# Inner weight sums split between GpSimd and VectorE, wide sums in other slots, and layer 1 mixed by ScalarE and GpSimd, in a two-level Strassen-Winograd kernel

## The chip, the cores and the metric

The kernel runs on one core of a Trainium2 chip. The metric is the time of one execution on the device in microseconds, lower is better; a kernel's time is the median of its runs. The profile is one more execution of the same program.

## The reference

The input x is 2 x 2048 x 512 in float32. Two layers are added to it, one after the other:

```python
def _L0_cond_ref(x, type_label, wi, wo, swi, swo, g1, g2):
    s0 = relu(x @ swi[0]) @ swo[0]
    s1 = relu(x @ swi[1]) @ swo[1]
    eo = relu(x @ wi[type_label]) @ wo[type_label]      # one of 3 experts per batch row
    gate_in = concat([eo[:, 0], s0[:, 0], s1[:, 0]], axis=-1)
    w = softmax(relu(gate_in @ g1) @ g2, axis=-1)       # 3 numbers per batch row
    return eo * w[0] + s0 * w[1] + s1 * w[2]

def _L1_cond_ref(x, cat_ids, W, b):
    return x @ W[cat_ids] + b[cat_ids]                  # one of 64 matrices per batch row

x = x + _L0_cond_ref(x, ...)
x = x + _L1_cond_ref(x, ...)
```

wi and swi are 512 x 2048, wo and swo 2048 x 512, g1 is 1536 x 512, g2 512 x 3, W 512 x 512. The gate reads the first row of a sequence alone.

## The kernel before

**Units.** The 4096 rows are cut into four blocks of 1024. A unit is one pair (weight set, block): units 0 to 3 are the first shared pair of matrices on blocks 0 to 3, units 4 to 7 the second, units 8 and 9 the expert of batch row 0 on blocks 0 and 1, units 10 and 11 the expert of row 1 on blocks 2 and 3. Every unit has an *up* half (x times wi, then relu, kept in SBUF as four quadrants H) and a *down* half (H times wo).

**Two levels of seven products.** Both halves use a Winograd variant of Strassen's method at two levels. At the outer level there are seven products i. Operand 1, 2 and 4 of a side are plain quadrants, 3, 5, 6 and 7 are sums of quadrants. Inside each product the same scheme is applied again with seven inner products k. In the up half an inner product is two slots (d = 0 and 1) of two matmuls each, in the order of `SEQ_UP`: x1 x1 y5 y5 x6 x6 z2 x7 x7 z2 x4 x4 y3 y3; the letter names the PSUM bank that it accumulates into. So an up half has 7 x 14 = 98 slots and a down half 7 x 7 = 49 slots of four matmuls each (`SLOTS_DN`). The outer order is 1, 6, 2, 5, 7, 4, 3 in an up half (1, 2, 6, 5, 7, 4, 3 in unit 0) and 1, 2, 3, 7, 6, 5, 4 in a down half. After a slot, VectorE or ScalarE takes what it needs out of the bank: a seed of z after x1 (`uz`, L614 and L616), a snapshot after x6 and x7 (`us`, L620 and L622; the bank goes on being accumulated, so x7 must wait for the snapshot of x6), results after the rest. Products 6, 2, 7, 4 and 3 add to a quadrant that is there already, on VectorE; 1 and 5 store, mostly on ScalarE.

**Sums beside the matmuls.** All of these are issued from one program in a fixed order (`tc.manual_schedule`), so each engine has a queue in program order:

- `x_sums` (L277 and L291, GpSimd): the sums of x of one product, made while the product before it runs.
- `wide` (L580 in product 7, L585 in product 4, VectorE): four sums of 128 x 1024 per product that add one quadrant of H to another; L585's results then get their relu on ScalarE.
- `make_tops` (L539 to L546) and `outer_sum` (L691), VectorE: sums of H for the down half.
- `prep_w` (L132, GpSimd): sums of weights of the next matrices. The seven matrices that follow the first one are prepared, one queued per unit in units 0 to 6. A matrix goes in four groups g: 1 MB is loaded into the one buffer `raw` (L165), four sums make `s` (outer sums, plain inner quadrants), four make `o` (plain outer, inner sums), four more make `t` from `s` (both), and each of the three is stored to DRAM (1 MB, tensors `ws`, L182), three steps later. `raw`, `s`, `o` and `t` have one buffer each.
- `fetch_w` (L374 to L393, SP): fetches weights of 256 KB, 12 ahead of their use, in order. Products of plain quadrants come from the inputs, others from `ws`. If the matrix is still being prepared, `ready` first issues all that is left of the preparation.

The background work is stepped from the slots: `paced(prep_bg, RATE_UP[n > 0][j])` and `paced(other_bg, 0.5)` after each up slot, 0.05 and 1 after each down slot.

**Layer 1 and the gate.** After unit 8 and after unit 10, `gate` computes the softmax weights (27 steps on `other_bg`). After units 8, 9 and 10, `layer1` is queued for the block just finished: it loads w1 (1 MB, L855) and the bias row (2 KB, `brow`, L857), multiplies the row by ones (`pb`, L865), and then handles eight tiles of 128 rows. Per tile it loads x and the three results (`mix`, four DMAs of 256 KB), adds the three with their gates on VectorE (L910), does four matmuls (`po`, L875) and adds the bias (L883). The `mix` tiles use the buffers raw, o and t in turn. The last block is done by `premix`, queued at the beginning of the last down half: it loads `acc` (2 MB) and four parts of 1 MB (`pm`, L939; the fourth when the first part's sums are issued), then weights and bias as above, then 16 sums (L947). At slot 47 of 49 what is left of it is issued at once; `last_mix` and `last_layer1` follow.

Of the kernel before, what the change touches and what calls it, by code (L numbers as in the profile page):

```python
# [32 lines left out]
def cond_resid_kernel(  # L33
# [101 lines left out]
    def prep_w(e, kind, eng):  # L135
# [3 lines left out]
        late = []  # L139

        def tick():
            for job in list(late):
                job[0] -= 1
                if job[0] <= 0:
                    job[1]()
                    late.remove(job)

        def load(g):
            t = bigp.tile([P, 2048], F32, tag="raw", bufs=1, name=f"pr_{e}_{kind}_{g}")
# [16 lines left out]
            return t  # L166

        raws = {0: load(0)}
        for _ in range(6):
            yield  # L170
        for g in range(NG):
            new = lambda part: bigp.tile(
                [P, 2048], F32, tag=part, bufs=1, name=f"p{part}_{e}_{kind}_{g}"
            )
            raw = raws[g].rearrange("p (a b c d f) -> p a b c d f", a=2, b=2, c=2, d=2)
            ts, to, tt = new("s"), new("o"), new("t")
            vs = ts.rearrange("p (s b d f) -> p s b d f", s=4, b=2, d=2)
            vo = to.rearrange("p (a c s f) -> p a c s f", a=2, c=2, s=4)
            vt = tt.rearrange("p (n s f) -> p n s f", n=4, s=4)

            def store(part, t, g=g):
                nc.sync.dma_start(  # L182
                    out=ws[e, kind, part][:, :, g * P : (g + 1) * P],
                    in_=t.rearrange("p (n f) -> p n f", n=16),
                )

            place = lambda n: SLOT_A[n] - 4
            for _ in sums_a(eng, lambda r, c: raw[:, r, :, c, :, :], lambda n: vs[:, place(n)]):
                tick()
                yield  # L190
            late.append([3, lambda t=ts, put=store: put("s", t)])
            for _ in sums_a(
                eng, lambda r, c: raw[:, :, r, :, c, :], lambda n: vo[:, :, :, place(n), :]
            ):
                tick()
                yield
            late.append([3, lambda t=to, put=store: put("o", t)])
            if g + 1 < NG:
                raws[g + 1] = load(g + 1)
# [6 lines left out]
        while late:  # L206
            tick()
            yield
# [874 lines left out]
```

## Time and profile before

| | |
|---|---|
| median of 3 runs | 2398.66 us (2397.9 to 2400.77) |
| the profiled execution | 2391.57 us |
| its span, first to last instruction | 2389.8 us |
| mean granted TensorE clock in it | 0.978 |
| DMA | 541.40 MB, mean 227 GB/s |

How to read it: PE is TensorE's matmuls, PEld its weight loads, DVE VectorE, ACT ScalarE, POOL GpSimd, SP the engine that issues nearly all DMAs (SPq is its queue). A line of the waits has the waiting engine and line, what it waited for, the sum in us, the number of times and the longest. A line of the windows has the stretch in us from the span's start, its length, the busy time and count of PE, PEld, DVE, ACT and POOL, the granted clock, the DMA engines' busy share and GB/s. A line of a timeline has the start, the duration, the engine, the line, the operation, output and inputs, shapes and count, and in brackets the idle time before it and what ended it. Each matmul of 32-bit floats has two records.

Unit n's halves in the span, read from the first and last matmul of each (us):

| unit | up from | down from | up | down |
|---|---|---|---|---|
| 0 | 15.5 | 147.5 | 131.5 | 93.0 |
| 1 | 240.4 | 335.2 | 95.0 | 88.7 |
| 2 | 423.7 | 516.5 | 92.9 | 89.6 |
| 3 | 605.9 | 697.1 | 91.4 | 85.3 |
| 4 | 782.3 | 877.5 | 95.3 | 85.3 |
| 5 | 962.6 | 1057.7 | 95.2 | 85.3 |
| 6 | 1142.8 | 1233.6 | 91.0 | 85.3 |
| 7 | 1318.7 | 1411.1 | 92.6 | 84.8 |
| 8 | 1495.7 | 1588.8 | 93.3 | 85.3 |
| 9 | 1674.0 | 1796.4 | 122.6 | 110.4 |
| 10 | 1906.7 | 2040.2 | 133.7 | 84.8 |
| 11 | 2124.8 | 2233.5 | 108.9 | 124.7 |

After unit 11 the last eight tiles of layer 1 take 31.6 us more. A half without any wait has 392 records of 0.216 us, 84.7 us; a tile of layer 1 adds 3.46 us. The up halves of units 9 and 11 hold three tiles of layer 1 and their down halves five, the up half of unit 10 holds eight.

### The profile page before, as it was taken

How to read it: one execution, taken by the hardware profiler on the slowest of the kernel's cores; microseconds unless marked ns; L12 is line 12 of the kernel's file. 1: busy time of each engine (PE TensorE's matmuls, PEld its weight loads, DVE VectorE, ACT ScalarE, POOL GpSimd, SP SyncE). 2: the span in 40 equal slices, each digit the busy share in tenths (PEclk: the TensorE clock that was granted, in tenths of full speed). 3: DMA queues.
4: the chain of work that ended last, by engine and by line, in shares of the span. 5: the costliest groups of instructions: out<-in, count | busy, mean ns of one | idle time of the engine just before them, and what ended most of it. 6: DMA issues, size and time to landing. Idle time of an engine off the chain costs nothing.

```text
span 2389.8 us, 28294 instructions
## 1 busy us (share of the span) xinstructions
PE 2232.5 (93%) x9808; PEld 1870.1 (78%) x9808; DVE 1725.6 (72%) x2082; ACT 500.4 (21%) x833; POOL 930.3 (39%) x774
## 2 busy tenths in 40 slices
PE   6879999989999999989999999999889989998979
PEld 5668888878878878878878878888666866886655
DVE  6857687587687687687687687687577557768755
ACT  3211221221221221221221321221221112112100
POOL 5932741741841861661841752752600320032000
PEclk9989999999999999999999999999999999999999
DMA  7775976976975985785975985785866565576662
GB/s 293 251 251 189 287 242 191 294 218 196 325 243 152 303 254 172 255 260 178 306 228 170 286 267 182 255 279 166 285 200 216 163 209 187 184 246 187 201 216 75
DMA packets 489784, 541.40 MB, mean 227 GB/s; under 512 B 25000, under 2 KB 326056, under 8 KB 486060
## 3 DMA queue, kind: packets, MB, share of 16 engines
q1 hardware_dynamic: 488588, 537.50, 70.4%
q10 hardware_dynamic: 1056, 2.10, 0.2%
q8 instruction: 80, 1.31, 0.2%
q14 instruction: 60, 0.49, 0.1%
HBM read 400.04 MB, written 139.46 MB: 226 GB/s over the span
## 4 chain that ended last, share of the span: by engine, by line
PE 66%; POOL 14%; DVE 9%; DMA 7%; issue 2%; SPq 2%; ACT 0%; POOLq 0%; ACTq 0%; DVEq 0%
PE dx L720 22%; PE ux L599 13%; PE dy L720 11%; PE uy L599 6%; PE dz L720 5%; PE po L875 5%; POOL ps L132 3%; POOL xi L291 3%; POOL po L132 3%; PE uz L599 3%; POOL pt L132 2%; DVE mix L910 1%; POOL x L277 1%; DMA xn<-in_x_dram 1%; DMA ws_t<-pt 1%
## 5 line engine op out<-in xcount | busy, mean ns | idle before, releaser
L599 PE MATMUL ux<-xi,w 128*128 128x256 f32 x1984 | 494.2, 391 | 72.7 <-issue 33.4
L599 PEld LDWEIGHTS ux<-xi,w 128*128 128x128 f32 x1984 | 382.9, 195 | 147.2 <-issue 53.0
L291 POOL TENSOR_TENSOR xi<-x 128x256 f32<-128x256 f32 x120 | 125.6, 1047 | 951.8 <-PE dx L720 928.2
L720 PE MATMUL dx<-t,w 128*128 128x256 f32 x1728 | 410.9, 381 | 1.7 <-DVE ds L742 1.5
L720 PEld LDWEIGHTS dx<-t,w 128*128 128x128 f32 x1728 | 328.0, 191 | 51.0 <-DVE ds L742 4.5
L622 DVE TENSOR_TENSOR us<-ux,h 128x512 f32<-128x512 f32 x240 | 162.4, 685 | 118.2 <-PE ux L599 118.1
L691 DVE TENSOR_TENSOR h<-h,h 128x1024 f32<-128x1024 f32 x192 | 229.1, 1217 | 0.0
L575 ACT ACTIVATE h<-h 128x1024 f32<-128x1024 f32 x156 | 164.7, 1056 | 294.5 <-DVE h L585 135.9
L633 ACT ACTIVATE h<-uz 128x512 f32<-128x512 f32 x168 | 99.5, 592 | 483.2 <-PE uz L599 458.2
L627 DVE TENSOR_TENSOR h<-uy,us 128x512 f32<-128x512 f32 x168 | 115.7, 691 | 89.9 <-ACT us L620 85.5
L599 PE MATMUL uy<-xi,w 128*128 128x256 f32 x672 | 162.3, 385 | 6.0 <-POOL xi L291 6.0
L720 PE MATMUL dx<-h,w 128*128 128x256 f32 x672 | 160.3, 382 | 0.5 <-DMA w<-in_L_cond_swo_dram 0.5
L720 PE MATMUL dy<-h,w 128*128 128x256 f32 x672 | 158.9, 379 | 0.5 <-DVE y L744 0.5
L720 PE MATMUL dz<-h,w 128*128 128x256 f32 x672 | 158.8, 379 | 0.0
L646 DVE TENSOR_TENSOR h<-uy,us 128x512 f32<-128x512 f32 x168 | 114.9, 690 | 56.9 <-PE uy L599 55.8
L599 PEld LDWEIGHTS uy<-xi,w 128*128 128x128 f32 x672 | 130.1, 194 | 26.1 <-POOL xi L291 6.4
L132 POOL TENSOR_TENSOR ps<-pr 128x512 f32<-128x512 f32 x56 | 81.8, 1471 | 168.7 <-DMA pr<-in_L_cond_wo_dram 49.0
L720 PEld LDWEIGHTS dx<-h,w 128*128 128x128 f32 x672 | 128.4, 192 | 19.3 <-issue 1.0
L720 PEld LDWEIGHTS dy<-h,w 128*128 128x128 f32 x672 | 127.4, 190 | 18.9 <-issue 1.0
L720 PEld LDWEIGHTS dz<-h,w 128*128 128x128 f32 x672 | 127.4, 190 | 17.2
L720 PE MATMUL dy<-t,w 128*128 128x256 f32 x576 | 136.1, 379 | 0.0
L599 PE MATMUL uz<-x,w 128*128 128x256 f32 x464 | 123.4, 390 | 0.0
(133 smaller groups left out, 3446.1 us busy)
## 6 DMA issues: line engine op xcount, KB each, us to landing
w<-ws_t SPq DMA_DIRECT2D x368, 256.0 KB, 3.4
w<-ws_s SPq DMA_DIRECT2D x282, 256.0 KB, 2.9
w<-ws_o SPq DMA_DIRECT2D x276, 256.0 KB, 3.7
ws_s<-ps SPq DMA_DIRECT2D x28, 1024.0 KB, 6.4
ws_o<-po SPq DMA_DIRECT2D x28, 1024.0 KB, 7.2
ws_t<-pt SPq DMA_DIRECT2D x28, 1024.0 KB, 7.1
ys<-y SPq DMA_DIRECT2D x11, 2048.0 KB, 7.9
w<-in_L_cond_swo_dram SPq DMA_DIRECT2D x72, 256.0 KB, 2.9
```

The source lines that it names most:

```text
L132: eng.tensor_tensor(o, i0, i1, op)
L277: eng.tensor_tensor(o[:, b], i0[:, b], i1[:, b], SUB)
L291: eng.tensor_tensor(s(k), i0, i1, SUB)
L575: nc.scalar.activation(v, v, AF.Relu)
L599: nc.tensor.matmul(p[:, g, :], lhsT=wt[:, 2 * d + g, :], rhs=x_ops[n, i, k], start=first and g == 0, stop=True, skip_group_check=True,)
L622: nc.vector.tensor_tensor(t, p, half(src, 12 if k == 6 else 22, d), ADD)
L627: nc.vector.tensor_tensor(half(dst, 22, d), bank["y", d], t, ADD)
L633: nc.scalar.activation(half(dst, 11, d), p, AF.Relu if i in final else AF.Copy)
L646: nc.vector.tensor_tensor(half(dst, 12, d), p, sn["b", d], ADD)
L691: nc.vector.tensor_tensor(bl(o), bl(i0), bl(i1), SUB)
L720: nc.tensor.matmul(p, lhsT=wt[:, g, :], rhs=op[g], start=first and g == 0, stop=True, skip_group_check=True,)
L875: nc.tensor.matmul(po[t], lhsT=mixed[:, c, :], rhs=l1[blk][0][:, c, :], start=(c == 0), stop=(c == DC - 1),)
```

## The change

- `prep_w` becomes a class `Prep` with two lines of jobs: p for GpSimd and d for VectorE. The sums of `o` go to VectorE in the preparations queued in units 1 to 6; `s` and `t` stay on GpSimd. The preparation queued in unit 0 stays whole on GpSimd and goes over its groups twice, first for `o` alone, then for `s` and `t`, so it loads each group twice. A d step is taken after up slots 2, 3 and 6 of products 1, 6, 2 and 3 and after down slots z2, y5 and x4 of products 6, 5 and 4, and not before 8 slots have passed since the group's load was issued. A group's load is issued when all jobs of the group before it have been.
- p steps follow new rates per slot, in up and in down halves.
- `ready` asks for one part (o, s or t) and no longer for the whole preparation; a part that is not complete is forced only when the weight is less than two uses away, and until then `fetch_w` stops there.
- `wide` moves from slots 1, 1, 3 and 5 to slots 1, 2, 5 and 11. In products 7 and 4 the x sums of the next product are issued from slot 7 on.
- `other_bg` is stepped after up slots 2, 3, 6, 9, 12 and 13 of each product (42 steps in an up half, 49 before), and after each down slot as before.
- In `layer1` the three results are scaled in place by ScalarE and added to x by GpSimd; tile t + 1 is mixed before the matmuls of tile t are issued. A block takes 59 steps, 47 before. The second tile is fetched after the weights are in. The lag before the weights are used is 10 steps, 6 before, here and in `premix`.
- The bias row's DMA is issued before that of w1.

```diff
-    def prep_w(e, kind, eng):
...
+    class Prep:
...
+        def __init__(self, e, kind, passes, d_eng):
+            self.e, self.kind, self.d_eng = e, kind, d_eng
+            self.todo = [(g, part) for part in passes for g in range(NG)]
+            self.left = {part: NG for part in "ost"}
+            self.p, self.d, self.late, self.reading, self.since = [], [], [], 0, 0
+
+        def begin(self):
+            if not self.todo:
+                return
+            g, parts = self.todo.pop(0)
...
+            self.since = clock[0]
+            raw = t.rearrange("p (a b c d f) -> p a b c d f", a=2, b=2, c=2, d=2)
...
+            def view(part):
+                if part not in own:
+                    self.flush(1 << 30, part)
+                    own[part] = bigp.tile(
+                        [P, 2048], F32, tag=part, bufs=1, name=f"p{part}_{e}_{kind}_{g}"
+                    )
...
+            def line(part, eng, pick, put):
+                gen = sums_a(eng, pick, put)
+
+                def op(k):
+                    next(gen)
+                    if part != "t":
+                        self.reading -= 1
+                    if k == 3:
+                        self.late.append((clock[0] + 3, part, g, own[part]))
+
+                return [lambda k=k: op(k) for k in range(4)]
...
+            if "s" in parts:
+                self.p += line(
+                    "s", nc.gpsimd, lambda r, c: raw[:, r, :, c], lambda n: view("s")[:, place(n)]
...
+                self.p += line(
...
+            if "o" in parts:
+                into = self.p if self.d_eng is nc.gpsimd else self.d
+                into += line(
+                    "o",
+                    self.d_eng,
...
+            self.reading = (4 if "s" in parts else 0) + (4 if "o" in parts else 0)
+
+        def flush(self, now, only="ost"):
+            for job in list(self.late):
+                due, part, g, t = job
+                if due > now or part not in only:
+                    continue
+                self.late.remove(job)
                 nc.sync.dma_start(
-                    out=ws[e, kind, part][:, :, g * P : (g + 1) * P],
+                    out=ws[self.e, self.kind, part][:, :, g * P : (g + 1) * P],
                     in_=t.rearrange("p (n f) -> p n f", n=16),
                 )
...
+        def step(self, line):
+            self.flush(clock[0])
+            jobs = self.p if line == "p" else self.d
+            if jobs and (line == "p" or clock[0] >= self.since + 8):
+                jobs.pop(0)()
+            self.more()
+
+        def more(self):
+            if self.reading == 0 and not self.p and not self.d:
+                self.begin()
...
+        def force(self, part):
+            self.more()
+            while self.left[part]:
+                if not (self.p or self.d):
+                    self.flush(1 << 30)
+                    continue
+                (self.p or self.d).pop(0)()
+                self.more()
+                if not (self.p or self.d):
+                    self.flush(1 << 30)
...
-    def ready(name):
-
-        while any(name == other for other, _ in prep_bg):
-            step(prep_bg)
-        return name in queued
+    clock = [0]
+    preps = {}
+
+    def ready(e, kind, part, need):
+
+        if (e, kind) not in preps:
+            return (e, kind) == (0, 0)
+        prep = preps[e, kind]
+        if prep.left[part] and need:
+            while prep_bg[0] is not prep:
+                for other in "ost":
+                    prep_bg[0].force(other)
+                prep_bg.pop(0)
+            prep.force(part)
+        return not prep.left[part]
...
             e = units[n][0]
-            if not ready((e, kind)):
+            si, sk = SLOT_A[i], SLOT_A[k]
+            part = ("t" if sk >= 4 else "s") if si >= 4 else "o" if sk >= 4 else None
+            if part and not ready(e, kind, part, w_next[0] < w_used[0] + 2):
                 return
...
-    pace = {}
-
-    def paced(bg, rate):
-        c = pace[id(bg)] = pace.get(id(bg), 0.0) + rate
-        while c >= 1:
-            step(bg)
-            c -= 1
-        pace[id(bg)] = c
+    def prep_step(line):
+        if prep_bg:
+            prep_bg[0].step(line)
+            if prep_bg[0].over():
+                prep_bg.pop(0)
+
+    pace = [0.0]
+
+    def prep_paced(rate):
+        clock[0] += 1
+        if prep_bg:
+            prep_bg[0].flush(clock[0])
+        pace[0] += rate
+        while pace[0] >= 1:
+            prep_step("p")
+            pace[0] -= 1
...
-                for cc in {1: (11, 22), 3: (21,), 5: (12,)}.get(s, ()):
+                for cc in {1: (11,), 2: (22,), 5: (21,), 11: (12,)}.get(s, ()):
                     wide(cc)
...
-                if j < 6 and not done and s % (2 if j else 1) == 0:
+                if j < 6 and not done and (
+                    s >= 7 if i in (7, 4) else s % 2 == 0 or j == 0
+                ):
                     done = advance(xg, 1)
                 if s in (2, 4, 6, 9):
                     next(tg, None)
-                paced(prep_bg, RATE_UP[n > 0][j])
-                paced(other_bg, 0.5)
+                prep_paced(RATE_UP[n > 0][j])
+                if s in (2, 3, 6) and i in (1, 6, 2, 3):
+                    prep_step("d")
+                if s in (2, 3, 6, 9, 12, 13):
+                    step(other_bg)
...
-            paced(prep_bg, 0.05)
-            paced(other_bg, 1)
+            prep_paced(RATE_DN[n > 0])
+            if i in (6, 5, 4) and name in ("z2", "y5", "x4"):
+                prep_step("d")
+            step(other_bg)
...
+        brow = small.tile([1, D], F32, tag="brow", name=f"brow_{blk}")
+        nc.sync.dma_start(out=brow, in_=bvec[bass.ds(cat[b], 1), :])
         w1 = bigp.tile([P, DC, D], F32, tag="s", bufs=1, name=f"w1_{blk}")
         nc.sync.dma_start(out=w1, in_=W_v[:, bass.ds(cat[b] * DC, DC), :])
-        brow = small.tile([1, D], F32, tag="brow", name=f"brow_{blk}")
-        nc.sync.dma_start(out=brow, in_=bvec[bass.ds(cat[b], 1), :])
...
-        fetch(0)
-        fetch(1)
-        yield from layer1_weights(blk, lag)
-        for t in range(NT):
+        def mix(t):
             m = mixed[t]
             for j in range(NX):
-                nc.vector.scalar_tensor_tensor(
-                    m[:, 3, :, :], m[:, j, :, :], gates[b][:, j : j + 1], m[:, 3, :, :],
-                    ALU.mult, ADD,
+                nc.scalar.activation(
+                    m[:, j, :, :], m[:, j, :, :], AF.Copy, scale=gates[b][:, j : j + 1]
                 )
+            yield
+            for j in range(NX):
+                nc.gpsimd.tensor_tensor(m[:, 3, :, :], m[:, 3, :, :], m[:, j, :, :], ADD)
                 yield
-            layer1_mm(blk, t, m[:, 3, :, :])
+
+        fetch(0)
+        yield from layer1_weights(blk, lag)
+        fetch(1)
+        yield from mix(0)
+        for t in range(NT):
+            if t + 1 < NT:
+                yield from mix(t + 1)
+            layer1_mm(blk, t, mixed[t][:, 3, :, :])
             yield
             if t + 2 < NT:
                 fetch(t + 2)
...
     RATE_UP = {
-        False: [0.6] * 7,
-        True: [0.3, 0.6, 0.6, 0.35, 0.15, 0.15, 0.6],
+        False: [0.3, 0.4, 0.4, 0.45, 0.45, 0.45, 0.6],
+        True: [0.3, 0.45, 0.45, 0.3, 0.1, 0.1, 0.35],
     }
+    RATE_DN = {False: 0.8, True: 0.14}
...
-                prep_bg.append((parts[n], prep_w(*parts[n], nc.gpsimd)))
-                queued.add(parts[n])
+
+                e0, k0 = parts[n]
+                preps[e0, k0] = Prep(e0, k0, ("o", "st"), nc.gpsimd) if n == 0 else Prep(
+                    e0, k0, ("ost",), nc.vector
+                )
+                prep_bg.append(preps[e0, k0])
...
-                        other_bg.append(("pre", premix(units[n][1], 6)))
+                        other_bg.append(("pre", premix(units[n][1], 10)))
...
-                    step(prep_bg)
+                    for part in "ost":
+                        prep_bg[0].force(part)
+                    prep_bg.pop(0)
...
-                    other_bg.append((f"l{blk}", layer1(blk, 6)))
+                    other_bg.append((f"l{blk}", layer1(blk, 10)))
```

## The prediction

> **What bounds the kernel now.** I read the busy shares first, then who TensorE waits for, then the windows of single products, and last the timelines of VectorE and GpSimd inside the products that run long.
>
> ```profile
> PE 2232.5 (93%) x9808; PEld 1870.1 (78%) x9808; DVE 1725.6 (72%) x2082; ACT 500.4 (21%) x833; POOL 930.3 (39%) x774
> ...
> PE ux L599 <- issue: 38.3, 18, 3.5
> PE ux L599 <- POOL xi L291: 24.5, 7, 12.4
> PE po L875 <- DVE mix L910: 24.3, 20, 2.2
> PE pb L865 <- DMA brow<-in_L_cond_b_dram: 16.5, 3, 9.2
> ```
>
> TensorE is the bound, so only its idle time and its slow-clock time can be won. The waits name short pieces; the windows show where they lie. Below is unit 5's up half: product 2 (an undisturbed one), then products 7 and 4, then the down half.
>
> ```profile
> 986.80:998.90 12.10, 12.10 (x58) 10.65 (x57) 8.13 (x12) 2.86 (x4) 7.92 (x8) 1.00 0.78 259
> 1011.00:1029.20 18.20, 15.30 (x58) 12.65 (x57) 15.88 (x16) 1.20 (x2) 18.20 (x16) 0.81 0.80 247
> 1029.20:1045.60 16.40, 12.82 (x58) 10.38 (x57) 15.60 (x16) 6.74 (x8) 16.24 (x12) 1.00 0.58 177
> 1057.70:1143.00 85.30, 85.04 (x394) 74.54 (x393) 67.39 (x75) 10.07 (x25) 22.45 (x17) 1.00 0.67 213
> ```
>
> A product costs TensorE 12.10 us (14 slots of 0.864). Products 7 and 4 take 18.2 and 16.4, with VectorE busy for 15.9 and 15.6 us and GpSimd without a pause; the down half has no loss. The same windows of units 1 to 8 give products 7 and 4 together 34.4, 32.3, 30.8, 33.2, 34.6, 30.0, 31.9 and 32.7 us: 259.9, which is 66.3 over 8 x 24.2. No other up product there is over 12.4 but one (13.6). Why they are slow:
>
> ```profile
> 1012.93 0.70 DVE L616 TENSOR_TENSOR uz<-ux,h 128x512 f32<-128x512 f32 x1 [0.23 <-PE ux L599]
> 1013.53 5.80 DVE L580 TENSOR_TENSOR h<-h,h 128x1024 f32<-128x1024 f32 x3
> 1019.26 1.28 DVE L622 TENSOR_TENSOR us<-ux,h 128x512 f32<-128x512 f32 x2
> ...
> 1020.04 2.47 PE L599 MATMUL ux<-xi,w 128*128 128x256 f32 x5 [2.90 <-issue]
> ...
> 1016.01 2.24 POOL L132 TENSOR_TENSOR pt<-pt,ps 128x512 f32<-128x512 f32 x1
> ...
> 1009.97 1.27 POOL L132 TENSOR_TENSOR pt<-ps 128x512 f32<-128x512 f32 x1
> ```
>
> Three wide sums (L580) stand in VectorE's queue ahead of the snapshot `us` that TensorE needs before x7; x7 starts as soon as that is done, so the wait called "issue" is this one. And the two engines take turns: a sum of two SBUF operands takes 1.27 us on GpSimd alone and 2.24 beside a wide one, the wide one 1.22 alone (L691's mean is 1217) and up to 2.3 beside GpSimd.
>
> **The change part by part.** The profiled execution took 2391.57 us (span 2389.8); the median of the runs is 2398.66, 7.1 more. I sum against the span and subtract from the median.
>
> *Wide sums spread, units 1 to 8.* Two of them now precede the snapshot instead of three, one comes after it, one at slot 11. Counting p steps and d steps slot by slot with the new rates, the eight GpSimd sums of a group fall into products 1, 6, 2 and early 5 in these units and none into 7 and 4. VectorE's queue in product 7, with 0.69 us per eviction (next start 0.60 later) and 1.22 per wide sum: seeds done at 2.5 us, two wide sums to 4.95, snapshot to 5.65; x7 can start at 6.05. No wait. The work is 12 x 0.60 + 4 x 1.22 = 12.1 us per product, equal to TensorE's; what spills over is taken up by product 3 (8.13 us busy). The moved x sums do not really move: nothing ties GpSimd to TensorE's slots, so eight of 0.73 us still run early in product 7 and push the snapshot by about 0.9 us. I leave 1.0 us per unit in products 7 and 4 together: 66.3 - 8 = 58 won. Bounds: 66, if all goes, and 18, if the contention stays.
>
> *Sums of o on VectorE.* 6 preparations x 4 groups x 4 = 96 sums of 128x512: 0.69 us each alone, up to 0.69 + 1.27 beside GpSimd; 66 to 188 us of VectorE, in products that have 4 us or more free. What can reach TensorE is product 2: in units 3 to 8 its three sums belong to a group whose load was issued 8 to 12 slots (7 to 10 us) before, and such loads (four DMAs of 256 KB on SP) landed 5.4 to 10 us after their first issue. VectorE takes its queue in order, so a late load holds the snapshot behind it, and GpSimd starts its own sums of that group at the same moment. If the load lands at 3.5 us into the product: two contended sums to about 7.1, snapshot 7.7, x7 late by 1.7 us. I charge 2 us in six units, 0.5 in two, 3 for the clock and half a microsecond as much again in product 6: 16 us. Bounds: 0 (loads always earlier) and 40 (5 us each). The o buffer's store (7.2 us to landing) is 10 slots ahead of its next use: the same order, in the same charge.
>
> *Unit 0.* It waits for GpSimd (114 of 147 us busy; x4 of product 3 waits 12.4 us behind the forced rest of the preparation). Forcing now happens only when a weight is two uses away, so 41 instead of 48 of its sums are issued in the up half. But two passes load each group twice (4 MB more), and in the first pass a load can only follow the fourth sum, so GpSimd stands about 5.5 us at four groups: 7 x 1.5 saved against 22 spent, the forced queue (12 us) saved, the spread wide sums save some 6 of its x7 waits (4.1 and 4.5 us in products 7 and 4), and at the start of down weights are fetched only 6 to 11 ahead while SP waits for late stores: 5 to 9 us. That is 10.5 - 22 + 12 + 6 - 7, net 0; bounds -15 and +20 (by the 12.4 us wait and 8 us around it).
>
> *Layer 1, units 9 to 11.* A tile's mix leaves VectorE (3 x 0.76) for three scalings on ScalarE (its nearest row is 0.59 for 128x512) and three sums on GpSimd (1.27 alone, 2.24 beside VectorE), one tile ahead of its matmuls, on engines that are busy for 21% and 39% of the span, GpSimd for less in these units. The 24.3 us of TensorE's waits for the mix go. What replaces them: the scalings are issued one step after their own loads (3.5 to 4.6 us to landing), so ScalarE stands about 2 us per tile, mostly away from the snapshots it owes; and 14 of a down half's 24 sums meet VectorE's outer sums, 1.2 us each: VectorE then has 65 us of work in 62. I charge 7 us per down half that holds eight tiles, 1.5 for one that holds four. Unit 9: up and down lose 27.4 and 8.4 us now; after, 12.5 (6 for weights queued behind three forced stores and the gate's 3.8 MB, plus slow clock) and 7: 16 won, bounds 0 and 28. Unit 10: 21.5 lost now, of which 7.0 is the bias row, which now has ten steps and a place ahead of 1 MB; after, 4.5: 17 won, bounds 10 and 20.
>
> One rule speaks against this part. The Trainium skill (GPSIMD Engine Reference, Engine selection) sends elementwise sums to VectorE because GpSimd needs about twice the time. The rows agree on the price: 1.27 against 0.76. By the rule the mix would cost 3 x 0.51 us more per tile, 37 us over 24 tiles, if it lay on the path; by the windows it does not.
>
> *The last unit.* Counting steps: before, layer 1 of the previous block ends at down slot 24, and the premix has slots 25 to 47. Now there are 42 steps in an up half instead of 49 and 59 + 27 to do instead of 47 + 27, so layer 1 ends at slot 43, the premix starts at 44 and is forced whole at 47. All of it moves past SP's last stores to the end: acc (2 MB), three loads of 1 MB, bias row, weights (1 MB), and 16 sums on VectorE.
>
> ```profile
> 2305.29 0.41 SPq L928 DMA_DIRECT2D acc<-xr  x1
> 2305.75 4.71 SPq L939 DMA_DIRECT2D pm<-ys  x3
> 2310.66 2.17 SPq L855 DMA_DIRECT2D w<-in_L_cond_W_dram  x1
> 2324.26 0.90 DVE L863 TENSOR_TENSOR w<-w,ident 128x128 f32<-128x128 f32 x4 [8.27 <-DMA w<-in_L_cond_W_dram]
> ```
>
> From the first issue the weights need 19 us. From then (T = 0): TensorE reaches the bias matmul at 7.8 and waits to 16; VectorE prepares weights and bias to 20.5, sums sixteen times 0.66 to 31.2, with the fourth load inside, and mixes; the last matmuls start at 32 instead of 9.5: 22.7 lost, 4 of slow clock, 7 for the tiles, against 22.7 that this down half loses now: 11 worse (bounds 0 and 22). Its up half wins 10 (13.8 now, 3.5 after). Net -1.
>
> Sum: 58 - 16 + 0 + 16 + 17 - 1 = 74. Time: 2398.66 - 74 = 2325 us.
>
> **The rivals.** *Less friction* (0.22): the loads land before VectorE asks (+16) and the unforced unit 0 keeps its 15: 2398.66 - 105 = 2294. For it: most loads land within 7.5 us. *The contention stays in products 7 and 4* (0.15), so that the move does not do what it says: GpSimd runs late behind its loads and its sums slide back under the wide ones; 18 instead of 58: 2365. For it: GpSimd works through 991 to 1047 us without a pause now; against: a third of the sums leave it. *Slower* (0.09): VectorE's in-order queue before the snapshots. If each of the 24 groups holds TensorE for 3.75 us (90 / 24) the whole gain is gone; at 5 us, which is what a load landing at 10 us and two contended sums make, it is 120 instead of 16: 2429. Against it: d steps stand at least 8 slots behind the load.
>
> **How the numbers follow.** My forecast has 0.52 with a range of its own of 2300 to 2350; 0.02 is left for no change. A difference under 0.2% (5 us) could not be told from none here. Faster 0.52 + 0.22 + 0.15 = 0.89, slower 0.09. The range 2280 to 2372 takes in most of the first two rivals and leaves out the slower one and the tails.
>
> **What would show it.** Right: products 7 and 4 of units 1 to 8 at 12 to 13.5 us; wide sums near 1.22 in them; no `po <- DVE mix`; a TensorE gap of 8 us before the last `pb` and one of about 12 before the last `po` matmuls. Wrong: gaps at x7 of product 2 above 3 us with VectorE waiting for `pr`; wide sums still at 2.2; up 0 over 140 us. If the last unit's end shows no second gap, that step is wrong; if ScalarE's scalings hold z or snapshots, layer 1 is.

## The result, and the profile after

The change makes the kernel slower by a little: 2405.79 us median (2401.01 to 2408.63, 8 runs) against 2398.39 us (8 runs on the same chip), ratio 1.0035, 95% interval 1.002 to 1.005. The forecast was 2325 us with 2280 to 2372. The profiled execution took 2406.3 us, span 2404.5, mean granted clock 0.969 (0.978 before). "Before" and "after" are the kernels without and with the change. By the medians the loss is 7.4 us; the tables below compare the two profiled executions, whose spans are 14.7 us apart, since the one of before was 7.1 us under its median.

By unit, from the first matmul of one to the first of the next (us):

| | before | after | change | forecast |
|---|---|---|---|---|
| unit 0 | 224.9 | 243.3 | +18.4 | 0 |
| units 1 to 8, products 7 and 4 | 260.1 | 206.2 | -53.9 | -58 |
| units 1 to 8, product 2 | 96.7 | 116.8 | +20.1 | +16 |
| units 1 to 8, down halves | 688.2 | 712.4 | +24.2 | 0 |
| unit 9 | 232.7 | 232.6 | -0.1 | -16 |
| unit 10 | 218.1 | 210.2 | -7.9 | -17 |
| unit 11 and the end | 262.1 | 275.7 | +13.6 | +1 |

The last row ends with VectorE's last sum.

The windows of unit 5: product 2, products 7 and 4, the down half (columns as in the windows before).

```profile
997.48:1014.78 17.30, 13.73 (x58) 11.58 (x57) 11.56 (x16) 2.94 (x4) 10.55 (x10) 0.90 0.62 221
1026.86:1039.64 12.78, 12.54 (x58) 10.48 (x57) 12.13 (x16) 1.20 (x2) 11.42 (x11) 1.00 0.91 292
1039.64:1051.80 12.16, 12.16 (x58) 10.56 (x57) 11.99 (x17) 5.66 (x7) 0.00 (x0) 1.00 0.49 145
1063.88:1154.70 90.82, 86.90 (x393) 75.33 (x392) 75.94 (x82) 10.11 (x25) 29.65 (x22) 0.98 0.72 223
```

Products 7 and 4 of this unit are within 0.7 us of the 12.10 that a product costs without any wait, and GpSimd does nothing in product 4. Product 2 and the down half have become the slow ones, both below clock 1.00. TensorE's waits, first the one of before that has grown, then those of after:

```profile
PE dx L720 <- DVE ds L742: 1.5, 6, 0.3
```

```profile
PE dx L788 <- DVE ds L810: 18.0, 9, 3.9
PE dx L788 <- ACT ds L808: 17.5, 5, 3.9
...
PE po L945 <- DVE acc L1035: 10.8, 1, 10.8
PE ux L662 <- POOL xt L323: 10.8, 1, 10.8
PE pb L935 <- DMA brow<-in_L_cond_b_dram: 10.3, 1, 10.3
```

Nothing in them names `mix` any more; what is new is `ds`, the down half's snapshot of a bank (as `us` is in the up half), made by VectorE or by ScalarE.

### The profile page after: what moved, and what is told of

The parts are those of the page before. It is cut to its first block, busy times and chain, and to the rows that moved or that the text cites. A ratio compares the mean times of both kernels' runs of the same rounds, so it can differ in the third digit from the quotient of the medians.

```text
span 2404.5 us, 28536 instructions
## 1 busy us (share of the span) xinstructions
PE 2243.9 (93%) x9808; PEld 1880.6 (78%) x9808; DVE 1778.1 (74%) x2106; ACT 544.5 (23%) x905; POOL 937.2 (39%) x750
## 4 chain that ended last, share of the span: by engine, by line
PE 70%; DMA 9%; POOL 9%; DVE 7%; SPq 3%; issue 2%; ACT 0%; POOLq 0%; ACTq 0%; DVEq 0%
PE dx L788 21%; PE ux L662 16%; PE dy L788 10%; PE uy L662 8%; PE dz L788 5%; PE po L945 5%; PE uz L662 4%; POOL xi L337 3%; DMA ws_o<-po 2%; DMA mix<-ys 2%; POOL ps L132 2%; DVE h L759 2%; POOL pt L132 2%; SPq L168 1%; POOL x L323 1%
## 5 line engine op out<-in xcount | busy, mean ns | idle before, releaser
L788 PE MATMUL dx<-t,w 128*128 128x256 f32 x1728 | 419.5, 386 | 32.1 <-DVE ds L810 18.0
L788 PEld LDWEIGHTS dx<-t,w 128*128 128x128 f32 x1728 | 330.8, 193 | 88.8 <-DVE ds L810 24.2
L132 POOL TENSOR_TENSOR ps<-pr_ost 128x512 f32<-128x512 f32 x48 | 72.6, 1524 | 545.0 <-DMA pr_ost<-in_L_cond_wo_dram 142.5
L337 POOL TENSOR_TENSOR xi<-x 128x256 f32<-128x256 f32 x120 | 114.0, 950 | 420.5 <-PE dx L788 396.6
L759 DVE TENSOR_TENSOR h<-h,h 128x1024 f32<-128x1024 f32 x192 | 252.2, 1337 | 0.0
L982 POOL TENSOR_TENSOR mix<-mix 128x512 f32<-128x512 f32 x72 | 118.9, 1652 | 301.9 <-ACT mix L977 291.6
L788 PE MATMUL dy<-h,w 128*128 128x256 f32 x672 | 164.3, 389 | 1.7 <-DVE y L812 1.7
```

The lines of the kernel that those rows point to most:

```text
L132: eng.tensor_tensor(o, i0, i1, op)
L337: eng.tensor_tensor(s(k), i0, i1, SUB)
L759: nc.vector.tensor_tensor(bl(o), bl(i0), bl(i1), SUB)
L788: nc.tensor.matmul(p, lhsT=wt[:, g, :], rhs=op[g], start=first and g == 0, stop=True, skip_group_check=True,)
L982: nc.gpsimd.tensor_tensor(m[:, 3, :, :], m[:, 3, :, :], m[:, j, :, :], ADD)
```

## The experiments

Each median is from four to six runs beside the kernel before on the same chip (its median was 2393 to 2396 us in them); the ratio is to that.

**1. The spread alone**, on the kernel before.

```diff
-for cc in {1: (11, 22), 3: (21,), 5: (12,)}.get(s, ()):
+for cc in {1: (11,), 2: (22,), 5: (21,), 11: (12,)}.get(s, ()):
...
-if j < 6 and not done and s % (2 if j else 1) == 0:
+if j < 6 and not done and (s >= 7 if i in (7, 4) else s % 2 == 0 or j == 0):
```

> The kernel before with two edits of the change alone: the wide sums at slots 1, 2, 5 and 11, and the x sums of products 7 and 4 from slot 7 on. Preparation, unit 0 and layer 1 are those of before. Theory (the spread alone won the 53 us that products 7 and 4 of units 1 to 8 lost between before and after, since only two wide sums are ahead of the snapshot that x7 needs): products 7 and 4 of units 1 to 8 sum to 200 to 212 us instead of 259.9, product 2 stays at 12.1 to 12.4, the down halves at 85 to 90, the time is 2398 - 50 to - 65 (unit 0 and units 9 to 11 have the two products too): 2333 to 2348 us. Rival (the 53 us needed GpSimd to be out of these products, which only the new rates and the o sums on VectorE did): GpSimd still runs through them, wide sums stay above 2 us, 18 of 66 us won, 2375 to 2385 us.

Measured: 2356.61 us, ratio 0.9832 (0.9819 to 0.9845). Products 7 and 4 sum to 228.2: 31.9 us won, between the two theories. The groups of wide sums, of before, of this kernel and then of after:

```profile
L580 DVE TENSOR_TENSOR h<-h,h 128x1024 f32<-128x1024 f32 x48 | 80.8, 1719 | 0.0
L585 DVE TENSOR_TENSOR h<-h,h 128x1024 f32<-128x1024 f32 x48 | 79.9, 1700 | 0.0
```

```profile
L585 DVE TENSOR_TENSOR h<-h,h 128x1024 f32<-128x1024 f32 x48 | 81.1, 1706 | 0.0
L580 DVE TENSOR_TENSOR h<-h,h 128x1024 f32<-128x1024 f32 x48 | 77.8, 1639 | 0.0
```

```profile
L643 DVE TENSOR_TENSOR h<-h,h 128x1024 f32<-128x1024 f32 x48 | 68.5, 1446 | 0.0
L648 DVE TENSOR_TENSOR h<-h,h 128x1024 f32<-128x1024 f32 x48 | 60.1, 1272 | 0.0
```

With the spread alone a wide sum is nearly as slow as before (1639 and 1706 ns, 1719 and 1700 before): the contention is still there, and 32 us come from one wide sum fewer ahead of the snapshot. The other 22 us of the change go with GpSimd's weight sums: in units 1 to 8 these fill 6.5 us of product 7 and 8.3 us of product 4 on average in this kernel, 0.9 and 0 in after, and the mean wide sum there falls from 1783 and 1859 ns to 1488 and 1234. The x sums stay in product 7. Experiment 12, which lowers the rates alone, wins 16.6 us of the same kind.

**2. The spread with the x sums where they were**: the first of the two edits above alone.

> The kernel before with the wide sums at slots 1, 2, 5 and 11 alone; the x sums of products 7 and 4 stay at every second slot from slot 0. Theory (nothing ties GpSimd to TensorE's slots, so a later place in its program order moves nothing, and the 32 us of the run with both edits come from two wide sums instead of three ahead of the snapshot): products 7 and 4 of units 1 to 8 at 225 to 232 us, the time within 5 us of 2356.6. Rival (a third or more of the 32 us came from x sums that no longer ran beside the wide ones): 238 us or more there, 2367 us or more.

Measured: 2355.2 us (0.9838, 0.9816 to 0.986), products 7 and 4 at 227.4. The x sums' new place is worth nothing, as expected.

**3. The o sums of after back on GpSimd.**

```diff
-                    e0, k0, ("ost",), nc.vector
+                    e0, k0, ("ost",), nc.gpsimd
```

> The kernel after with one edit: the o sums of all seven preparations on GpSimd, so that VectorE's queue holds none of them; rates, parts, unit 0's two passes, wide slots and layer 1 are those of after. Theory (VectorE's queue waits for the group's load and for the store of the o buffer, and holds what TensorE needs): product 2 of units 1 to 8 falls from 116.8 to 97 to 100 us, the down halves of units 1 to 8 from 713.7 to 690 to 697, products 7 and 4 stay near 206: 2406 - 35 to - 45, 2361 to 2371 us. Rival (in the down halves it is GpSimd's own sums, whose rate went from 0.05 to 0.14 per slot, that slow VectorE's tops and outer sums): product 2 wins its 18 us, the down halves keep 18 or more of their 24, and products 7 and 4 lose 5 to 15 to the third more sums on GpSimd: 2390 to 2400 us.

Measured: 2406.26 us (1.0044, 1.0031 to 1.0058), the time of after. Product 2 is at 96.7 and the down halves fall to 696.0, so 36.5 us come back; but products 7 and 4 go up to 241.1 and eat it. At these rates the o sums cost the same on either engine, in other places. The rival named these places, but with 5 to 15 us for products 7 and 4 where 34.9 came.

**4. Layer 1's load ahead of the mix**, in after.

```diff
+            if t + 2 < NT:
+                fetch(t + 2)
             if t + 1 < NT:
                 yield from mix(t + 1)
             layer1_mm(blk, t, mixed[t][:, 3, :, :])
             yield
-            if t + 2 < NT:
-                fetch(t + 2)
```

> The kernel after with one edit: in layer 1 the load of tile t + 2 is issued before the mix of tile t + 1 instead of behind tile t's matmuls, so that a tile's scalings come six steps behind its load instead of one. Theory (ScalarE stood 67.8 us for its own loads, and the snapshots, seeds and d results queued behind those scalings held TensorE): the scalings' wait falls below 15 us, the waits of the down matmuls for ds and dz (about 40 us in sum, of which some are not layer 1's) halve, the down halves of units 9, 10 and 11 fall from 128.5, 105.1 and 140.5 to about 115, 95 and 128: 2406 - 25 to - 35, 2371 to 2381 us. Rival (GpSimd's mix sums beside VectorE's outer sums are the cost, ScalarE's wait is beside the path): the scalings wait less, but the three down halves lose less than 6 us together, 2400 us or more.

Measured: 2368.91 us (0.9897, 0.9881 to 0.9912), 36.9 less than after. The down halves of units 9 and 10 and the last one with the end: 112.2, 98.3 and 168.0 (after: 128.3, 104.9 and 182.0). What it took away, on ScalarE and TensorE in unit 9's down half of after:

```profile
1853.36 0.72 ACT L977 ACTIVATE mix<-mix,g 128x512 f32<-128x512 f32 x1 [5.18 <-DMA mix<-ys]
1854.60 1.53 ACT L977 ACTIVATE mix<-mix,g 128x512 f32<-128x512 f32 x2 [0.52 <-DMA mix<-ys]
1856.04 0.36 ACT L808 ACTIVATE ds<-dx 128x256 f32<-128x256 f32 x1
```

```profile
1856.45 3.67 PE L788 MATMUL dx<-t,w 128*128 128x256 f32 x8 [3.51 <-ACT ds L808]
1859.92 1.95 PE L788 MATMUL dy<-h,w 128*128 128x256 f32 x8
```

ScalarE stands 5.18 us for the tile's load, scales three times, and only then copies the `ds` that TensorE has been waiting for. TensorE loses 3.51 us, and then 1.7 more at half speed: the next eight records (four matmuls) take 3.67 us, the eight behind them 1.95. The scalings' group, of after and then of this kernel (the idle time before the scalings stands behind the second bar):

```profile
L977 ACT ACTIVATE mix<-mix,g 128x512 f32<-128x512 f32 x72 | 50.2, 718 | 67.8 <-DMA mix<-ys 66.1
```

```profile
L977 ACT ACTIVATE mix<-mix,g 128x512 f32<-128x512 f32 x72 | 46.4, 711 | 0.0
```

**5. Unit 0's preparation as before**, in after: one pass, before's rates, the rest issued when the first weight of it is 12 uses away.

```diff
-preps[e0, k0] = Prep(e0, k0, ("o", "st"), nc.gpsimd) if n == 0 else Prep(
+preps[e0, k0] = Prep(e0, k0, ("sot",), nc.gpsimd) if n == 0 else Prep(
...
-        if prep.left[part] and need:
+        if prep.left[part] and (need or prep.one):
...
-        False: [0.3, 0.4, 0.4, 0.45, 0.45, 0.45, 0.6],
+        False: [0.6] * 7,
...
-    RATE_DN = {False: 0.8, True: 0.14}
+    RATE_DN = {False: 0.05, True: 0.14}
```

> The kernel after with unit 0's preparation as before: one pass over the groups (s, o, t, the next load issued once s and o are), all sums on GpSimd at 0.6 per up slot and 0.05 per down slot, and the rest issued at once when the first weight of it is to be fetched, 12 ahead. All else is after's. Theory (two passes load each group twice and wait for the o buffer's store, so that GpSimd's x sums stand behind it and late stores hold the fetches): unit 0 takes 216 to 226 us instead of 243.3 (before 224.9, less some us for the spread wide sums): 2406 - 17 to - 27, 2379 to 2389 us. Rival (unit 0 is longer for VectorE's wide sums or the other rates, and the second pass is hidden): unit 0 stays over 236 us, 2398 us or more.

Measured: 2371.29 us (0.9896, 0.9881 to 0.9911), 34.5 less than after. Unit 0 takes 221.0 us, 22.3 less, as the theory has it. The other 10 or so (31.9 us by the profiled executions) are in units 1 to 11: product 2 falls by 8.5, the down halves of units 1 to 8 rise by 6.7, and units 9 to 11 take 7.9 less. They were not followed.

**6. Two buffers in unit 0's first pass**, in after, with both passes kept.

```diff
-t = bigp.tile([P, 2048], F32, tag="raw", ...)
+odd = parts == "o" and g % 2
+t = bigp.tile([P, 2048], F32, tag="s" if odd else "raw", ...)
...
-    [P, 2048], F32, tag=part, ...
+    [P, 2048], F32, tag="t" if odd else part, ...
...
-if self.reading == 0 and not self.p and not self.d:
+if self.reading == 0 and not self.p and not self.d or self.first and len(self.p) <= 4:
```

> The kernel after with one edit in unit 0's first pass: two buffers in turn for the loads (raw and s) and for the o sums (o and t), and the next group's load is issued when four sums are left instead of none. Both passes, the rates and the rest stay. Theory (the second pass itself is hidden; unit 0 is longer because in the first pass GpSimd stands 8.2, 6.8 and 8.4 us for a load issued behind the last sum and a store behind that, with the x sums in its queue behind): those waits go, the up half falls from 139.0 to 120 to 126 us, the down half from 104 to about 98: 2406 - 15 to - 22, 2384 to 2391 us. Rival (16 more loads and the late stores on SP hold x, the weights and the fetches, whenever they are issued): less than 6 us won, 2400 us or more.

Measured: 2381.51 us (0.9935, 0.9916 to 0.9953). The up half falls by 23.1, from 139.0 to 115.9 us, below before's 132.0, with two passes; the down half stays at 104.6. GpSimd and SP in after, and the sum of such waits:

```profile
40.74 1.60 POOL L132 TENSOR_TENSOR po<-pr_o,po 128x512 f32<-128x512 f32 x1
42.30 1.27 POOL L323 TENSOR_TENSOR xt<-x 128x512 f32<-128x512 f32 x1
51.76 1.26 POOL L132 TENSOR_TENSOR po<-pr_o 128x512 f32<-128x512 f32 x1 [8.19 <-DMA ws_o<-po]
52.97 1.26 POOL L323 TENSOR_TENSOR xt<-x 128x512 f32<-128x512 f32 x1
```

```profile
42.36 1.76 SPq L168 DMA_DIRECT2D pr_o<-in_L_cond_swo_dram  x4
44.16 0.62 SPq L225 DMA_DIRECT2D ws_o<-po  x1
```

```profile
POOL po L132 <- DMA ws_o<-po: 23.4, 3, 8.4
```

The load and the store start when the group's fourth sum is done, GpSimd stands 8.19 us for them, and the x sum `xt` that TensorE waits 10.8 us for is behind the wait. The down half's 11 us are SP's: its x loads wait behind the second pass's stores, and TensorE's transposes for them (waits of 7.5, 1.8 and 3.6 us here). That is read from the trace and was not tried.

**7. Experiments 4 and 5 together**, in after.

> The kernel after with both edits of the two runs before: layer 1's load of tile t + 2 ahead of the mix of tile t + 1, and unit 0's preparation as before. Theory (the two costs are separate, each at its own place: 36.9 us for the fetch, 34.5 us for unit 0): 2405.8 - 71.4 = 2334 us, in the range of the forecast; unit 0 at 221 us, the down halves of units 9, 10 and 11 at 112, 98 and 168 (with the end). Rival (a good part of either number is something common, the clock or DMA traffic): they overlap by 10 us or more, 2345 to 2355 us.

Measured: 2338.64 us (0.9768, 0.9752 to 0.9784). Unit 0 takes 220.2, units 9 and 10 take 215.4 and 200.7. The two costs are separate but for 4 us: 67.2 less than after, where experiments 4 and 5 add up to 71.4.

**8. Before with the spread and the change's layer 1**, with experiment 4's order; all weight sums on GpSimd, in before's order and rates.

> The kernel before with the spread (as in the first run) and the change's layer 1 with its load issued ahead of the mix: scalings on ScalarE, sums on GpSimd, bias row first, lag 10, 42 steps per up half. All weight sums stay on GpSimd, unit 0 included, in before's order and at before's rates. Theory (o sums on VectorE and the rates that go with them lose more in product 2 and in the down halves than the 22 us they win in products 7 and 4; layer 1 is worth 16, 17 and 3 us in units 9, 10 and 11 against the run with the spread alone): 2356.6 - 36 = 2321 us, units 1 to 8 at 715 us up and 689 down. Rival (the change's preparation with unit 0 undone is as good as before's): no better than the kernel with both edits undone, 2334 us or more.

Measured: 2325.78 us (0.971, 0.9694 to 0.9727), 13 less than experiment 7. The halves of units 1 to 8 sum to 715.0 and 689.5; in experiment 7 to 704.7 and 713.7. So the change's way of preparing weights in these units is a net loss.

**9. The premix early**, on experiment 8.

```diff
-                if s in (2, 3, 6, 9, 12, 13):
+                if s in (2, 3, 6, 9, 12, 13) or n == 11 and s in (0, 4, 8, 10):
```

> The kernel of the line above with one more edit: in unit 11's up half the gate and layer 1 get ten steps per product instead of six, 70 for 42, so that layer 1 ends near slot 16 of the last down half and the premix starts there and not at slot 44. Theory (the two TensorE gaps at the end, 10 us before the bias matmul and 11 us before the last tiles, stand only because the premix is started late and issued at once; the slow clock behind them goes as well): 18 to 26 us less than the line above, 2295 to 2303 us. Rival (16 sums, the weights and 7 MB of loads then lie beside the last down half's outer sums and weights and hold those): under 10 us less, or none.

Measured: 2309.84 us (0.9642, 0.9625 to 0.9659), the best kernel of the study: 3.6% below before. Both gaps at the end are gone; the last down half with the end falls from 168.0 to 133.8, and unit 11's up half, where the steps went, rises from 92.4 to 107.6.

**10. Its mix back on VectorE**, on experiment 9: before's three `scalar_tensor_tensor` per tile and before's order of the loop, so a tile is mixed right before its own matmuls and no longer one tile ahead, and a block takes 47 steps. The rest is kept.

> The kernel of 2309.8 us (spread, all weight sums on GpSimd, early premix) with the mix of layer 1 back on VectorE, three scalar_tensor_tensor per tile, 47 steps a block; bias row first, the lag of 10, 42 and 70 steps and the order of the loads stay. Theory (the engine is what counts: VectorE is full in these halves, 24.3 us of TensorE's waits named its mix, and moving it won the 16 and 17 us of units 9 and 10): 20 to 35 us slower, 2330 to 2345 us, the waits for the mix back at 15 to 24 us. Rival (the bias row, the later weights and loads ahead of use were the gain): within 8 us of 2309.8.

Measured: 2353.54 us (0.9824, 0.9806 to 0.9842), 43.7 slower, more than expected. What the engine and what the lost lead of one tile cost is not told apart by this run. The wait is back:

```profile
PE po L878 <- DVE mix L913: 28.6, 18, 2.8
```

**11. Other places for the sums of units 1 to 6**, on experiment 7 with experiment 9's edit.

```diff
-            if jobs and (line == "p" or clock[0] >= self.since + 8):
+            if jobs and (line == "p" or clock[0] >= self.since + 14):
...
-                if s in (2, 3, 6) and i in (1, 6, 2, 3):
+                if s in (2, 3, 6) and i in (1, 6, 2, 5, 3):
...
-            if i in (6, 5, 4) and name in ("z2", "y5", "x4"):
+            if i in (6, 5) and name in ("z2", "y5", "x4"):
...
-        True: [0.3, 0.45, 0.45, 0.3, 0.1, 0.1, 0.35],
+        True: [0.4, 0.6, 0.6, 0.35, 0.1, 0.1, 0.6],
...
-    RATE_DN = {False: 0.05, True: 0.14}
+    RATE_DN = {False: 0.05, True: 0.05}
```

> The kernel after with unit 0's preparation as before, the fetch ahead of the mix, ten steps per product in unit 11's up half (all three as in the runs above), and new places for the weight sums of units 1 to 6: d steps in products 1, 6, 2, 5 and 3, 14 slots after the load instead of 8, none in product 4 of the down halves, and p steps at 0.4, 0.6, 0.6, 0.35, 0.1, 0.1, 0.6 in up halves and 0.05 in down halves. The sums are the same on the same engines. Theory (what o on VectorE cost was a matter of place: the load late for product 2, GpSimd's sums beside the tops and outer sums of down product 2, the o buffer's store late for down product 4): against 2338.6 less 16 for the premix, product 2 gives 9 to 12 us and the down halves 20 to 25: 2286 to 2295 us, better than the 2309.8 of the kernel with all sums on GpSimd. Rival (sums on VectorE beside busy GpSimd cost what they cost wherever they stand, the wait moves to products 6, 5 or 3): 2308 us or more.

Measured: 2340.6 us (0.977, 0.9753 to 0.9788): the theory falls as a whole and holds in its down part. In units 3 to 8 every down half is back at 84.7 to 85.2 (unit 1's is 98.5, 88.5 before). The up halves rise to 759.0: product 2 is at 125.2, product 5 at 113.8, products 7 and 4 at 229.3, and in unit 1 VectorE's sums in product 5 wait 7.2 us and hold TensorE for 9.2. Product 2 in unit 5:

```profile
995.69 1.27 POOL L132 TENSOR_TENSOR ps<-pr_ost 128x512 f32<-128x512 f32 x1 [12.51 <-DMA w<-ws_o]
```

```profile
1003.59 3.32 DVE L132 TENSOR_TENSOR po<-pr_ost 128x512 f32<-128x512 f32 x2 [3.44 <-DMA w<-ws_t]
```

GpSimd has used the load from 995.69 on, so VectorE waits 3.44 us for something else than the load. What is left is the one o buffer, whose last store began to be issued at 992.44 and took 5.05 us in that. A second o buffer does not fit in SBUF and was not tried, so that cause is argued, not shown.

**12. Lower rates before products 7 and 4**, on experiment 9.

```diff
-        True: [0.3, 0.6, 0.6, 0.35, 0.15, 0.15, 0.6],
+        True: [0.35, 0.35, 0.35, 0.2, 0.05, 0.05, 0.75],
...
-            paced(prep_bg, 0.05)
+            paced(prep_bg, 0.15 if n else 0.05)
```

> The kernel of 2309.8 us (spread, all weight sums on GpSimd, the change's layer 1 with the early fetch, early premix) with one edit: the rates of the weight sums from unit 1 on, per slot of products 1, 6, 2, 5, 7, 4, 3: 0.35, 0.35, 0.35, 0.2, 0.05, 0.05, 0.75 instead of 0.3, 0.6, 0.6, 0.35, 0.15, 0.15, 0.6, and 0.15 per down slot instead of 0.05. Theory (what is left of the loss in products 7 and 4, 229.4 us against 193.6 without any wait, is GpSimd running late out of products 6, 2 and 5, where its sums and the x sums need more than the product's 12.1 us): products 7 and 4 of units 1 to 8 fall to 205 to 215 us, the down halves lose 0 to 8: 2290 to 2303 us. Rival (GpSimd's sums beside the tops and outer sums cost in the down halves, as in the change, and the x sums alone keep products 7 and 4 slow): 2306 us or more, the down halves 10 to 24 us longer.

Measured: 2373.83 us (0.9915, 0.9892 to 0.9938). The sums did not get done in time: what was left at the end of unit 8 was issued at once, and unit 9's second product waits 57 us for its x sums behind it: the rates were sized too low. Beside that, in units 1 to 8 products 7 and 4 fall to 212.8, 16.6 won, product 5 rises by 11.3 to 109.1, and the down halves rise to 710.3, 21.7 lost. Down product 2 of unit 7, on VectorE, GpSimd and TensorE:

```profile
1408.83 1.95 DVE L694 TENSOR_TENSOR h<-h,h 128x1024 f32<-128x1024 f32 x1
1410.71 2.29 DVE L539 TENSOR_TENSOR t<-h 128x1024 f32<-128x1024 f32 x1
1413.10 2.10 DVE L542 TENSOR_TENSOR t<-h,t 128x1024 f32<-128x1024 f32 x1
1415.12 0.41 DVE L745 TENSOR_TENSOR ds<-dx,y 128x256 f32<-128x256 f32 x1
```

```profile
1407.45 2.25 POOL L132 TENSOR_TENSOR po<-po,pr 128x512 f32<-128x512 f32 x1
1409.78 2.13 POOL L132 TENSOR_TENSOR po<-pr,po 128x512 f32<-128x512 f32 x1
1411.88 4.45 POOL L132 TENSOR_TENSOR pt<-ps 128x512 f32<-128x512 f32 x2
```

```profile
1415.59 1.65 PE L723 MATMUL dx<-t,w 128*128 128x256 f32 x3 [3.52 <-DVE ds L745]
```

No sum of o is on VectorE here. Beside GpSimd's sums alone the outer sum (L694) and the tops (L539, L542) take 1.95 to 2.29 us, where their means before are 1.22 and 1.25 to 1.27, and the `ds` behind them is 3.52 us late. After has the same in down product 2 of unit 6, with a gap of 2.96 us.

## Why the prediction was wrong

The sum was 74 us of gain; the profiled executions show 14.7 us of loss (the medians 7.4). The 89 us between them lie in three steps.

**"Unit 0 ... net 0": 18 us.** The term "GpSimd stands about 5.5 us at four groups" (22 us) had about the right sum: GpSimd stands 8.2, 6.8 and 8.4 us, since the store is issued behind the load and the next sum needs both, and with these waits gone experiment 6 is 23.1 us shorter in the up half. What was too large is what the prediction set against them: 10.5 + 12 + 6 us saved, where the up half of experiment 6 is only 16.1 us under before's. The 6 us for the spread wide sums did not come in this half (experiment 1 has it at 133.9, before at 132.0). That is 12 us, and 4 more are the start of the down half: "5 to 9 us", 7 in the sum, was 11.4. The bound of +20 covered it all; the middle did not.

**"On engines that are busy for 21% and 39%": 38 us** (units 9, 10, 11: 16, 9 and 13). The step that failed is "ScalarE stands about 2 us per tile, mostly away from the snapshots it owes". It stands 66.1 / 24 = 2.75 us per tile, and the three scalings behind the load hold `ds` and `dz`; the prediction had named this itself as a sign of being wrong. With experiment 4 units 9, 10 and 11 change by -16.5, -17.8 and -1.7 against before; the forecast was -16, -17 and +1. That the rest of the step comes out so well is in part luck. The 7 and 1.5 us charged for GpSimd's mix sums beside VectorE's outer sums do not show: the down halves of units 9 and 10 take 112.2 and 98.3 us there, no more than 84.7 and 3.46 for each of their eight and four tiles. The up half of unit 9 loses 19.3 us instead of 12.5, that of unit 11 7.7 instead of 3.5. The two gaps at the end held (10.3 and 10.8 us for 8 and 12). An engine's share of busy time says nothing of what stands behind a wait in its queue.

**Units 1 to 8: 33 us, of which 24 are down halves charged at nothing.** The prediction counted eight GpSimd sums per group out of products 7 and 4 and did not follow them and VectorE's d steps into the down halves. Of the 24.2 us, 11.0 are in down product 2 and 11.6 in down product 4. In product 2 the sums meet VectorE's tops and outer sums (experiment 12 shows it without o sums on VectorE), and the d steps of product 4 wait in VectorE's queue ahead of `ds`; with the d steps gone in experiment 3, product 4 is 11.2 us shorter and product 2 5.1. In unit 5 of after, product 4:

```profile
1144.07 1.66 DVE L132 TENSOR_TENSOR po<-pr_ost 128x512 f32<-128x512 f32 x1 [2.27 <-issue]
1145.65 3.41 DVE L765 TENSOR_TENSOR y<-y 128x512 f32<-128x512 f32 x2
1148.99 0.41 DVE L810 TENSOR_TENSOR ds<-dx,y 128x256 f32<-128x256 f32 x1
```

TensorE stands 3.88 us for that `ds`. In experiment 11, where both causes are taken out, the two products are back at their times before.

**What held.** Products 7 and 4 (58 forecast, 54 measured; only unit 1's product 7 stays slow, 17.1 us), the x sums that "do not really move" (experiment 2), and product 2 (16 forecast, 20 measured) by the mechanism described. Its size is partly luck: units 3 to 8 lose 0.3 to 5.2 us each, not 2. In unit 5 the load is in use from 6.7 us into the product instead of 3.5, and the lead of 7 to 10 us was not there: SP began to issue the load at 997.02, and VectorE reached its sums at 1000.18:

```profile
1004.19 2.36 DVE L132 TENSOR_TENSOR po<-pr_ost 128x512 f32<-128x512 f32 x2 [4.02 <-DMA w<-ws_s]
1006.48 1.27 DVE L685 TENSOR_TENSOR us<-ux,h 128x512 f32<-128x512 f32 x2
```

```profile
1004.23 3.45 POOL L132 TENSOR_TENSOR ps<-pr_ost 128x512 f32<-128x512 f32 x2 [18.72 <-DMA pr_ost<-in_L_cond_wo_dram]
```

**The rivals.** The slower rival named VectorE's queue before the snapshots, from 90 us up; it cost 20, and the slowdown came from places that no rival named. GpSimd's sums did leave products 7 and 4, but their cost mostly changed its place: in experiment 12, with all of them on GpSimd, 16.6 us won there stand against 21.7 lost in the down halves.

The rule of the Trainium skill that was weighed (GPSIMD Engine Reference, Engine selection: elementwise sums belong on VectorE, since GpSimd is about twice as slow) would have put the mix back on VectorE; experiment 10, which does so and gives up the lead of one tile, is 43.7 us slower. The rule prices the sum; the runs price the queue.

## What to carry to other kernels

When work is moved to another engine, follow every moved instruction to its new place in that engine's queue, write down what it waits for there, and what owed to the bound engine stands behind it; a share of busy time answers neither. A wait for a load in an in-order queue can be cured by issuing the load several steps earlier; two kernels that differ only in that are 37 us apart here. Before a change of several parts is dropped, build it from its parts: here two of them with an earlier load and a better pace give 3.6%, and the third, the split of the weight sums, is what to leave out in both of the places tried (experiments 7 and 11).

## What the runs showed of the hardware

A TensorE gap has a price beyond its length, and a size from which it is charged. Take the gaps over 0.6 us ahead of a record of 256 columns in units 1 to 11 of four profiles (before, after, experiments 1 and 9), and count among the 20 records behind it those of 256 columns that start 0.36 to 0.52 us after the one before, instead of 0.216. Behind the 61 gaps of up to 1.93 us there is one such at most; behind 22 of the 36 gaps from 1.96 to 3.12 us, and behind all 12 from 3.2 us up, there are 5 to 14, each some 0.2 us. So the five gaps of 3.4 to 3.6 us cost 4.6 to 6.1 each, and ten gaps of 1 us cost ten. The Trainium skill (TensorE: Matmul & The Clock Gate, Part 1) says the clock is halved after an idle window of about 3.4 us; the gaps above that agree, but most gaps of 2 to 3 us are charged here too, and the measurement decides.

A bias row of 2 KB, issued ahead of the 1 MB of weights but behind four loads of 5 MB in all, still lands late at the end of after: it is issued at 2341.55 us, and TensorE, which waits for it, starts at 2354.39, 12.8 us later. Before, behind the weights as well, it was 10.8 us (2313.01 to 2323.80), so the place ahead of that one load shows no gain here.
